# Layer 1 of a four-layer image network on Trainium2: norm sums from 32-column tiles, roots through DRAM rows, and one fold moved from VectorE to GpSimd

## The chip, the cores and the metric

The kernel runs as one program on 1 core of one Trainium2 chip. The metric is device time in microseconds (us) of that core; the number that counts is the median of the runs. Engines are named as in the profile: PE (TensorE matmuls), PEld (its weight loads), DVE (VectorE), ACT (ScalarE), POOL (GpSimd) and SP (SyncE, which issues nearly all DMAs here).

## The reference, cut to what matters

Sixteen images of 96 channels and 56 x 56 pixels pass four layers. Only layer 1 is touched. B = 16, C = 96, Din = 192, L = 3136 pixels.

```
z  = transpose(x)                              # pixels x channels
u  = LN(z) * g + b;  u = u @ in_proj_w.T       # norm 1, 96 -> 192 channels
uc = silu(depthwise_conv3x3(u))
# four directions k: rows, columns, and both reversed
dt = softplus(dts @ dt_w + dt_b);  a = exp(dt * A)
h  = scan(a, dt * B * x)                       # h[t] = a[t] h[t-1] + ...
y  = h * C + D * x
ym = y0 + reverse(y2) + turn(y1 + reverse(y3)) # "turn" swaps rows and columns
z  = z + LN(ym) @ out_proj_w.T                 # out norm, 192 -> 96
m  = LN(z);  z = z + gelu(m @ fc1 + b1) @ fc2 + b2
out = x + z
```

Each of the three norms subtracts a mean over the channels and divides by a root of a variance over the channels.

## The kernel before, in words

Layer 1 is written as small generator tasks. Each step yields an `Op` with an engine, an estimated cost, and the buffers it takes and gives; `in_order` then places the steps one by one, always the one that could start first by these estimates, ties by a rank. The result is a fixed order of instructions on every engine; on the chip each engine works through its own order and waits on semaphores where its operands aren't ready. SP's and POOL's queues are such orders too.

Five task families run beside each other over the 16 images. `front` (rank 3b - 9) makes the first norm, the projection, the convolution (L1107) and the step projections (`p_x`, L1144, whose copy to `proj` at L1146 marks the end of a front). `made_of` (rank -100) makes the step sizes: `p_d` (L1174) on PE, then three ACT passes (L1181, L1183, L1190), and loads the rows `bc` (L1203). `scanned` (rank 99) is DVE's backbone: for 24 pieces of 784 columns a product (L1262), a product into PSUM (L1265), a scan (L1271 or L1273) and a product with C (L1226), and for a third of them L1229. `additions` (rank -1) adds the pieces on POOL (L1295). `back` (rank 3b) makes the out norm, the output projection, the second norm and the MLP in 7 groups of 448 pixels.

The steps that the change touches:

- Norm 1 (`sums` in `front`): per 448 pixels the pixels are the *weights* and a 96-column block of ones is streamed, so that a pixel's sum lies on its own partition (L1035 for x, L1036 for its square from L1029; DVE picks one column, L1038). After L1044 and L1045 POOL takes the power -1/2 (L1047, 112x28). The root is turned back to rows by 28 transposes with a broadcast root as weights (L1057), and DVE multiplies x by it (L1062).
- Channels 128 to 191 of two directions share one tile: partitions 0 to 63 hold rows, 64 to 127 the turned direction. At the end of `sums` of `scanned`, four DVE additions fold the turned half in (L1300, 64x784 each).
- Out norm (`group` in `back`): squares on ACT (L1317, L1319), then per 112 pixels `p_o` from the image as weights: the projection (L1324, L1325, whose 97th column is the mean) and the sum of squares against 96 columns of ones (L1327). ACT copies `p_o` (L1332), DVE makes the variance (L1340, L1341), POOL the root (L1343, 112x4), DVE multiplies (L1350) and adds `p_y` = x + bias (L1347, L1352).
- Second norm: ACT squares (L1357), DVE sums z (L1359) and the squares (L1361), POOL takes the root (L1366). After the MLP, `p_g` (L1392, L1393) is added (L1395) and SP writes 112 x 4 rows of 384 bytes (L1397).

An fp32 matmul appears as two records in the profile, each with a weight load of its own; a transpose as one.

Of the kernel before, what the change touches and what calls it, by code (L numbers as in the profile page):

```python
# [163 lines left out]

class Phase:
# [60 lines left out]
def in_order(buffers, tasks, load=None):  # L226
# [8 lines left out]
    def advance(ready, task, parent, root):  # L235
        nonlocal count
        while True:
# [9 lines left out]
            elif isinstance(got, list):  # L247
                up = [task, len(got), parent, ready]
                for child in got:
                    advance(ready, child, up, root)  # L250
                return
            elif isinstance(got, int):
                ranks[root] = got
            else:
                waiting.append((ready, ("ps" not in got.give, ranks[root], count), task, parent, got, root))
                count += 1
                return
# [3 lines left out]
    while waiting:  # L261
        best = None
        for i, (ready, rank, _, _, op, _) in enumerate(waiting):
            start = max(ready, engines.get(op.engine, 0.0))
            if op.engine == "ACT" and op.table and op.table != tables.get("ACT"):
                start = max(ready, engines.get("ACT", 0.0) + change["ACT"])
# [5 lines left out]
            if best is None or (start, rank) < best[:2]:  # L272
                best = (start, rank, i)
        start, _, i = best
        assert start < np.inf, "the tasks hold all buffers"
        _, _, task, parent, op, root = waiting.pop(i)
# [560 lines left out]
def layer1(ctx, tc, src, given, dst, flags=None, soft=False):  # L837
# [6 lines left out]
    buffers = {  # L844
        "ps": 3, "x": 1, "half": 1, "xc": 2, "big": 7, "proj": 2, "dt": 3, "a": 2, "bc": 3, "hc": 1, "xn": 1,
        "ysq": 1, "o": 2, "z": 2, "zn": 2, "zt": 1, "hid": 1, "xr": 3,
    }
# [28 lines left out]
    ones = ph.c([P, 3, C], "ones")  # L876
# [57 lines left out]
    for i in range(2):  # L934
# [11 lines left out]
        rows.append(ph.c([C1, C], f"rows{i}"))  # L946
        nc.vector.tensor_copy(rows[i], p[:C1, 0, :C])
# [4 lines left out]
    nc.vector.memset(w_out[:, 0, C:], 1.0 / DIN)  # L952
    nc.vector.memset(w_out[:64, 1, C:], 1.0 / DIN)
    for j, n in enumerate((P, 64)):
# [5 lines left out]
        nc.vector.tensor_copy(w_out[:n, j, :C], p[:n, 0, :C])  # L960
    b_fc1 = ph.c([P, 3], "b_fc1")
# [28 lines left out]
    def pe(n, each, take=("ps",), give=(), **k):  # L990
        return Op("PE", n * each, 0.25, take, give, **k)

    def dve(n, each=1.04e-3, over=0.15, **k):
        return Op("DVE", over + n * each, **{"lag": 0.06, **k})

    def act(n, each=0.83e-3, over=0.22, **k):
        return Op("ACT", over + n * each, **k)

    def front(b, it):

        def loaded(g):
            n = min(896, L - 896 * g)
            x = buf([C, 896], "xc")[:, :n]
            nc.sync.dma_start(x, given[b][:, 896 * g : 896 * g + n])
            return x
# [15 lines left out]
        me = work.tile([Q, 8, NT], F32, tag="me", name="me")  # L1021

        def sums(g):
            yield Op("SP", 0.3, 4.0, take=("xc",))
            x = loaded(g)
            for i in range(x.shape[1] // T):
                yield act(T, take=("xn",))
                sq = buf([C, 2, T], "xn")[:, 0]
                nc.scalar.activation(sq, x[:, T * i : T * i + T], AF.Square)  # L1029
                last = i == x.shape[1] // T - 1  # L1030
                yield pe(8, 0.2, give=("xn", "xc") if last else ("xn",))
                p = pair("p_s", P)
                for q in range(4):
                    at = T * i + Q * q
                    nc.tensor.matmul(p[:Q, q, :C], x[:, at : at + Q], ones[:C, 0], start=True, stop=True)  # L1035
                    nc.tensor.matmul(p[:Q, 4 + q, :C], sq[:, Q * q : Q * q + Q], ones[:C, 0], start=True, stop=True)  # L1036
                yield dve(8, give=("ps",))
                nc.vector.tensor_copy(me[:, :, 2 * g + i : 2 * g + i + 1], p[:Q, :, 0:1])  # L1038

        yield [sums(g) for g in range(4)]  # L1040
        v, r = (work.tile([Q, 28], F32, tag=n, name=n) for n in ("v", "r"))
        yield dve(0, over=0.6)
        own = lambda a: a.rearrange("p (g q) -> p q g", q=4)
        nc.vector.scalar_tensor_tensor(own(v), me[:, :4], -1.0, me[:, :4], ALU.mult, ALU.mult)  # L1044
        nc.vector.scalar_tensor_tensor(own(v), own(v), EPS, me[:, 4:], ALU.add, ALU.add)  # L1045
        yield Op("POOL", 6.2)
        nc.gpsimd.tensor_tensor(r, v, nhalf, ALU.pow)  # L1047

        def projected(g):
            banks = 2 if g < 3 else 1  # L1050
            yield Op("SP", 0.3, 4.0, take=("xc",))
            x = loaded(g)
            yield pe(4 * banks, 0.1, ("ps", "xn"))
            p = pair("p_r")
            for q in range(4 * banks):
                at = 8 * g + q
                nc.tensor.transpose(  # L1057
                    p[:C, q // 4, Q * (q % 4) : Q * (q % 4) + Q], r[:, at : at + 1].to_broadcast([Q, C]), ident[:Q, :Q]
                )
            yield dve(448 * banks, give=("ps", "xc"))  # L1060
            xn = buf([C, 2, T], "xn")[:, :banks]
            nc.vector.tensor_tensor(xn, x.rearrange("c (b n) -> c b n", n=T), p[:C, :banks, :T], ALU.mult)  # L1062
# [148 lines left out]
    def scanned(it):  # L1211
# [66 lines left out]
        def sums():  # L1278
            for unit in units:
# [4 lines left out]
                for s in ((1, 0) if back else (0, 1)):  # L1284
# [9 lines left out]
                    yield Op("POOL", 1.9, give=("hc",))  # L1294
                    nc.gpsimd.tensor_tensor(out, out, hc, ALU.add)  # L1295
            ym = it["y"][1]
            for g in range(4):
                yield dve(L / 4, 1.85e-3)
                own = image(ym[:64])[:, 14 * g : 14 * g + 14]
                nc.vector.tensor_tensor(own, own, turned(ym[64:])[:, 14 * g : 14 * g + 14], ALU.add)  # L1300

        it["sums"] = sums()
        yield from scan()

    def back(b, it):

        y0, ym = it["y"]

        def group(g):
# [5 lines left out]
            yield act(T, take=("ysq",))  # L1315
            sq = buf([P, 2, T], "ysq")
            nc.scalar.activation(sq[:, 0], y0[:, cols], AF.Square)  # L1317
            yield act(T)
            nc.scalar.activation(sq[:, 1], ym[:, cols], AF.Square)  # L1319
            yield pe(16, 0.2, ("ps", "o"), ("ysq",))  # L1320
            p = pair("p_o", P)
            for q in range(4):
                own = slice(T * g + Q * q, T * g + Q * q + Q)
                nc.tensor.matmul(p[:Q, q, :C1], y0[:, own], w_out[:, 0], start=True, stop=False)  # L1324
                nc.tensor.matmul(p[:Q, q, :C1], ym[:, own], w_out[:, 1], start=False, stop=True)  # L1325
                for j in range(2):
                    nc.tensor.matmul(  # L1327
                        p[:Q, 4 + q, :C], sq[:, j, Q * q : Q * q + Q], ones[:, 1 + j], start=j == 0, stop=j == 1
                    )
            yield act(4 * C)  # L1330
            o = buf([Q, 4, C1], "o")
            nc.scalar.copy(o, p[:Q, :4, :C1])  # L1332
# [4 lines left out]
            small = lambda n: work.tile([Q, 4], F32, tag=n, name=n, bufs=3)  # L1337
            v, r = small("v4"), small("r4")
            yield dve(0, over=0.4, give=("ps",))
# [538 lines left out]
```

## Time and profile before

| what | value |
|---|---|
| runs (us) | 7140.94, 7140.69, 7134.35; median 7140.69 |
| profiled execution | 7114.45 us, its span 7112.6 us |
| layer 1 in the trace | first sums at 1164.0 us, last output DMA issued at 4417.1 us |
| ends of the fronts (L1146), first and last of 16 | 1281.6 us and 4085.3 us |
| the same in the settled part: six ends, five distances | 2958.9 us to 3897.6 us, so 187.7 us an image |
| granted PE clock over the span | 0.92 |

A busy share is that of the whole span, over four layers. For this change only layer 1 counts, about 3250 us of the span, and in it the settled part from 2200 us to 3950 us, where every image repeats the same order. [...]how fast PE gets on is read from the distance between the starts of neighbouring records.

### The profile page before, as it was taken

To read this page: it belongs to the slowest core of one execution; us is meant where nothing else is said; L and a number is where in the kernel's file an instruction comes from. 1 tells how busy PE (TensorE), PEld (TensorE's weight loads), DVE (VectorE), ACT (ScalarE), POOL (GpSimd) and SP (SyncE) were. 2 spreads that over 40 slices of the span, in tenths; PEclk is the share of its full clock that TensorE was granted. 3 is DMA by queue.
4 is the path that set the end of the run, shared out by engine and by line. 5 is a ranking of instruction groups with operands and counts; after the bars stand their busy time and mean duration, and the time that the engine had idled before them with its cause. 6 is when DMAs were issued, how large, how long until landed. Compare 5 with 4: busy or idle time off the path is not lost. (4 is left out here: it accounts for less than half of the span.)

```text
span 7112.6 us, 114994 instructions
## 1 busy us (share of the span) xinstructions
PE 6280.9 (88%) x46587; PEld 4500.6 (63%) x46587; DVE 5446.3 (77%) x7392; ACT 4546.6 (64%) x6035; POOL 1446.6 (20%) x994
## 2 busy tenths in 40 slices
PE   7999998888889999999999987788999999999986
PEld 3444444445655655556555555687888888888875
DVE  6786884677888888888888885667777777777775
ACT  4454542676777777777777763455666666666664
POOL 0000000132323333333333332111111111111110
PEclk9999998788899999999999988899999999999997
DMA  1111111343444444444444442445555455555542
GB/s 38 31 38 32 40 33 38 110 123 117 124 127 124 127 127 130 127 137 127 128 131 130 126 122 76 96 107 125 130 115 126 112 128 118 121 135 118 119 105 61
DMA packets 495422, 743.56 MB, mean 105 GB/s; under 512 B 199969, under 2 KB 330785, under 8 KB 491570
## 3 DMA queue, kind: packets, MB, share of 16 engines
q1 hardware_dynamic: 493858, 733.25, 39.9%
q8 instruction: 370, 6.06, 0.4%
q0 software_dynamic: 1024, 2.85, 0.1%
q14 instruction: 170, 1.39, 0.1%
HBM read 543.98 MB, written 191.99 MB: 103 GB/s over the span
## 5 line engine op out<-in xcount | busy, mean ns | idle before, releaser
L1578 POOL TENSOR_TENSOR r<-v,nhalf 112x16 f32<-112x16 f32 (+1 forms) x128 | 397.0, 3108 | 2241.5 <-DVE v L1576 1680.7
L1295 POOL TENSOR_TENSOR big<-big,hc 128x784 f32<-128x784 f32 x256 | 537.2, 2099 | 901.9 <-DVE hc L1226 815.2
L1262 DVE TENSOR_TENSOR dt<-dt,big 128x784 f32<-128x784 f32 x384 | 505.5, 1317 | 176.9 <-ACT a L1190 176.7
L777 DVE SCALAR_TENSOR_TENSOR h<-pad,rows,h 128x1568 f32<-128x1568 f32 x288 | 525.9, 1844 | 3.9
L1174 PE MATMUL p_d<-proj,l_dt 32*128 32x392 f32 x1536 | 388.3, 590 | 96.6 <-ACT hid L1384 69.1
L1181 ACT ACTIVATE dt<-p_d,l_dtb 128x784 f32<-128x784 f32 x384 | 350.0, 912 | 128.2 <-PE p_d L1174 110.6
L1636 PE MATMUL p<-k_f,z 112*128 112x112 f32 x3072 | 373.9, 282 | 63.9 <-DMA z<-d 57.5
L1636 PEld LDWEIGHTS p<-k_f,z 112*128 112x128 f32 x3072 | 369.2, 198 | 72.4 <-issue 59.1
L1684 PE MATMUL p_v<-w,gg 128*112 128x97 f32 x2048 | 377.3, 267 | 38.3 <-DVE gg L1670 12.3
L1107 PE MATMUL p_c<-x,taps 64*64 64x392 f32 x4608 | 400.7, 498 | 3.7 <-ACT big L1128 2.7
L1265 DVE TENSOR_TENSOR drive<-dt,bc 128x784 f32<-128x784 f32 x384 | 395.0, 1029 | 11.1 <-DMA bc<-bc 1.0
L1392 PE MATMUL p_g<-l_fc,hid 128*112 128x96 f32 x2688 | 386.1, 285 | 11.8 <-ACT hid L1384 9.4
L1128 ACT COPY big<-p_c 64x392 f32<-64x392 f32 (+1 forms) x448 | 267.3, 599 | 189.7 <-PE p_c L1107 184.1
L1392 PEld LDWEIGHTS p_g<-l_fc,hid 128*112 128x112 f32 x2688 | 347.2, 200 | 51.0 <-ACT hid L1384 24.6
L1685 PE MATMUL p_v<-w2both,gg 128*112 128x97 f32 x2048 | 375.5, 266 | 0.0
L1226 DVE TENSOR_TENSOR hc<-a,bc 128x784 f32<-128x784 f32 x384 | 371.3, 967 | 0.3 <-POOL big L1295 0.2
L1183 ACT ACTIVATE dt<-dt,one 128x784 f32<-128x784 f32 x384 | 363.6, 947 | 7.2
L1382 PE MATMUL p_f<-zt,w_fc 96*128 96x448 f32 x672 | 320.1, 594 | 47.6 <-ACT dt L1181 18.8
L1190 ACT ACTIVATE a<-dt,aneg 128x784 f32<-128x784 f32 x384 | 352.1, 939 | 4.5 <-DVE a L1273 3.1
L750 PE MATMUL p_c<-pad,taps 64*64 64x392 f32 x4032 | 348.8, 495 | 1.8 <-DVE y L816 1.4
L1273 DVE TENSOR_TENSOR_SCAN a<-a,drive 128x784 f32<-128x784 f32 x192 | 350.3, 1824 | 0.1
L1271 DVE TENSOR_TENSOR_SCAN a<-a,drive 128x784 f32<-128x784 f32 x192 | 350.0, 1823 | 0.0
(339 smaller groups left out, 16005.2 us busy)
## 6 DMA issues: line engine op xcount, KB each, us to landing
bc<-bc SPq DMA_DIRECT2D x256, 784.0 KB
bc<-bc SPq DMA_DIRECT2D x256, 392.0 KB
d<-y SPq DMA_DIRECT2D x448, 192.0 KB
z<-d SPq DMA_DIRECT2D x128, 672.0 KB
d<-uu SPq DMA_DIRECT2D x256, 169.8 KB
z<-d SPq DMA_DIRECT2D x192, 194.0 KB
xc<-x SPq DMA_DIRECT2D x96, 336.0 KB
x<-in_x SPq DMA_DIRECT2D x16, 1176.0 KB
```

The source lines that it names most:

```text
L777: nc.vector.scalar_tensor_tensor(out, view, taps9[:, i : i + 1], out, ALU.mult, ALU.add)
L1107: nc.tensor.matmul(p[to : to + 64, b, :TC], taps[64 * s : 64 * s + 64, j, k], pad[64 * s : 64 * s + 64, r0 : r0 + 7, k % 3 : k % 3 + S], s ...
L1174: nc.tensor.matmul(p[:, b, :TC], wdt[on, i], proj[on, h], start=True, stop=True)
L1226: nc.vector.tensor_tensor(hc, a, t[:, 1], ALU.mult)
L1262: nc.vector.tensor_tensor(as_own(dt), as_own(dt), own(u), ALU.mult)
L1265: nc.vector.tensor_tensor(b, dt, t[:, 0], ALU.mult)
L1295: nc.gpsimd.tensor_tensor(out, out, hc, ALU.add)
L1392: nc.tensor.matmul(p[:Q, q, :C], hid[:, j, own], fc2[:, j], start=j == 0, stop=False)
L1578: nc.gpsimd.tensor_tensor(r, v, nhalf[:, :n], ALU.pow)
L1636: nc.tensor.matmul(p[:, q, :Q], flat[:, P * (3 * q + k) : P * (3 * q + k) + P], f2, start=True, stop=True)
L1684: nc.tensor.matmul(out, gs[2 * h][:, at + k], w["w2"][:, 2 * h], start=True, stop=False)
L1685: nc.tensor.matmul(out, gs[1][:, at + k], w["w2both"][:, h], start=False, stop=True)
```

## The change

What it does:

- Norm 1 becomes a task family of its own (`normed`). The ones are now the *weights*, 32 columns wide, and the pixels are streamed: four matmuls, each into another 32 partitions of PSUM, take four quarters of 896 pixels. ACT squares the mean, DVE subtracts it from the mean square (`spread`), a DMA writes one partition of each quarter to a row in DRAM. When a whole image's row is there, it is loaded as 112 x 28, POOL takes the power, and it is written back as a row. In `front` a DMA broadcasts 896 roots to 96 partitions, and the 28 transposes are gone.
- The out norm's sums are made the same way for a whole image (`spreads`, four pieces of 784 pixels, from 128 and then 64 partitions), with one load, one POOL power of 112 x 28 for an image, instead of 7 of 112 x 4. `p_o` holds the projection alone; its pixels are taken four apart (`each`), so that a partition holds four neighbouring pixels and the roots come in pieces of 16 bytes. The image's pixels `x` are taken in the same way for `p_y` and `p_g`. The output is written in pieces of 1536 bytes.
- The 97th column of the weights now holds their row sums, so that the sum of z comes with the products and DVE's sum (L1359) is gone, as is ACT's copy (L1332).
- The fold of the turned half is made by POOL, piece by piece, as soon as a piece is complete; a DMA first moves 64 x 784 values from partitions 64 to 127 to partitions 0 to 63.
- The planner gets leads for some pairs of engine and task (subtracted from or added to a step's start when the next one is chosen), other ranks, slightly changed estimates and other numbers of buffers.

The diff, cut to its core:

```diff
+TUNED = {'layer1': {'buffers': {... 'xn': 1, 'ysq': 1, 'vr': 1, 'fold': 1, 'xr1': 1, 'z': 2, 'zn': 1, 'xr': 2},
+            'leads': {('PE', 'spreads'): -1.4, ('PE', 'steps'): -3.4, ('SP', 'sums'): -0.4, ('ACT', 'hidden'): -0.7,
+                      ('SP', 'norms'): 2.5, ('POOL', 'fronts'): -0.9, ('POOL', 'backs'): -0.6, ('SP', 'projected'): -2.9,
...
+            'hold': 0.3, 'norm': -6, 'front': -6, 'back': -3, 'make': -100, 'scan': -50, 'chains': 3}}
...
-            if best is None or (start, rank) < best[:2]:
-                best = (start, rank, i)
+            if best is None or (start + key, rank) < best[:2]:
+                best = (start + key, rank, i, start)
...
-    ones = ph.c([P, 3, C], "ones")
+    ones = ph.c([P, 3, 32], "ones")
...
     def pe(n, each, take=("ps",), give=(), **k):
-        return Op("PE", n * each, 0.25, take, give, **k)
+        return Op("PE", 1.05 * n * each, 0.25, take, give, **k)
...
+    def spread(mean, square, out, n):
+        yield act(n, take=("vr",))
+        t = buf([P, 224], "vr")[:, :n]
+        nc.scalar.activation(t, mean, AF.Square)
+        yield dve(n, give=("ps",))
+        nc.vector.scalar_tensor_tensor(t, t, -1.0, square, ALU.mult, ALU.add)
+        yield Op("SP", 0.3, 3.0)
+        nc.sync.dma_start(out.rearrange("o (q n) -> (o q) n", q=4), t[::32])
...
+        def sums(g):          # in normed
...
+            for k, a in enumerate((x, sq)):
+                for q in range(4):
+                    nc.tensor.matmul(p[32 * q : 32 * q + 32, k, :n], ones[:C, 0], a[:, n * q : n * q + n], start=True, stop=True)
+            yield from spread(p[:, 0, :n], p[:, 1, :n], var[:, 896 * g : 896 * g + 4 * n], n)
+        yield [sums(g) for g in range(4)]
...
+        nc.sync.dma_start(v, whole_of(var))
+        nc.vector.tensor_scalar(v, v, EPS, None, ALU.add)
+        nc.gpsimd.tensor_tensor(r, v, nhalf, ALU.pow)
+        nc.sync.dma_start(whole_of(it["root"]), r)
...
         def projected(g):
-            for q in range(4 * banks):
-                nc.tensor.transpose(p[:C, q // 4, Q * (q % 4) : Q * (q % 4) + Q], r[:, at : at + 1].to_broadcast([Q, C]), ident[:Q, :Q])
+            nc.sync.dma_start(rb, it["root"][:, 896 * g : 896 * g + n].to_broadcast([C, n]))
+            nc.vector.tensor_tensor(xn.rearrange("c b n -> c (b n)"), x, rb, ALU.mult)
...
-            for g in range(4):
-                yield dve(L / 4, 1.85e-3)
-                nc.vector.tensor_tensor(own, own, turned(ym[64:])[:, 14 * g : 14 * g + 14], ALU.add)
+        def folded():
+            for k in (3, 2, 1, 0):
+                yield Op("none", 0.0, 0.0, wait=folds[k])
+                yield Op("SP", 0.3, 3.0, take=("fold",))
+                nc.sync.dma_start(t, ym[64:, SUB * k : SUB * k + SUB])
+                yield Op("POOL", 1.9, give=("fold",))
+                nc.gpsimd.tensor_tensor(own, own, t.rearrange("p (w h) -> p w h", h=S), ALU.add)
...
+        def spreads(g):       # in back
+            nc.scalar.activation(sq, y0[:, cols], AF.Square)
+            nc.scalar.activation(ym[64:, cols], ym[:64, cols], AF.Square)
+            yield pe(4, n * 1.7e-3, give=("ysq",))
+            for k, (full, part, on) in enumerate(((y0[:, cols], ym[:64, cols], slice(0, 64)), (sq, ym[64:, cols], slice(64, P)))):
+                for i in range(2):
+                    for q in range(4):
+                        nc.tensor.matmul(p[32 * q : 32 * q + 32, k, :n], (ones[:, 1], ones[on, 1])[i], (full, part)[i][:, own], start=i == 0, stop=i == 1)
+            yield from spread(p[:, 0, :n], p[:, 1, :n], var[:, cols], n)
...
+        nc.gpsimd.tensor_tensor(r2, v2, nhalf, ALU.pow)
+        each = lambda t, q: t.rearrange("c (p q) -> c q p", q=4)[:, q]
...
-                nc.tensor.matmul(p[:Q, q, :C1], y0[:, own], w_out[:, 0], start=True, stop=False)
-                nc.tensor.matmul(p[:Q, q, :C1], ym[:, own], w_out[:, 1], start=False, stop=True)
-                for j in range(2):
-                    nc.tensor.matmul(p[:Q, 4 + q, :C], sq[:, j, Q * q : Q * q + Q], ones[:, 1 + j], start=j == 0, stop=j == 1)
-            nc.scalar.copy(o, p[:Q, :4, :C1])
+                nc.tensor.matmul(p[:Q, q, :C1], each(y0[:, cols], q), w_out[:, 0], start=True, stop=False)
+                nc.tensor.matmul(p[:Q, q, :C1], each(ym[:64, cols], q), w_out[:64, 1], start=False, stop=True)
...
-                nc.tensor.matmul(p[:Q, q, :C], x[:, Q * q : Q * q + Q], rows[0], start=True, stop=True)
+                nc.tensor.matmul(p[:Q, 4 + q, :C1], each(x, q), rows[0], start=True, stop=True)
...
-            nc.vector.tensor_reduce(s1, z, AX.X, ALU.add)
...
-                nc.tensor.matmul(p[:Q, q, :C], x[:, own], rows[1], start=False, stop=True)
+                nc.tensor.matmul(p[:Q, q, :C], each(x, q), rows[1][:, :C], start=False, stop=True)
...
-        in_order(buffers, [fronts(), makes(), scans(), additions(), backs()], None if soft else one_set)
+        in_order(buffers, [norms(), fronts(), makes(), scans(), additions(), backs()], None if soft else one_set, tuned["hold"], tuned["leads"])
```

## The prediction

> **What bounds the kernel now.** I read four views in this order. First the slices of the page. Each slice is 178 us; layer 1 fills slices 7 to 25.
>
> ```profile
> PE   7999998888889999999999987788999999999986
> DVE  6786884677888888888888885667777777777775
> PEclk9999998788899999999999988899999999999997
> ```
>
> PE stands at nine tenths, DVE at eight: PE is nearest to full, DVE next. Then the windows of the settled part (us, then busy us with instructions for PE, PEld, DVE, ACT, POOL, then PE clock, DMA share, GB/s).
>
> ```profile
> 2800.00:2990.00 190.00, 175.44 (x1338) 114.21 (x1338) 165.14 (x203) 148.46 (x195) 65.50 (x48) 0.93 0.45 128
> 2990.00:3180.00 190.00, 174.84 (x1334) 113.76 (x1335) 165.31 (x200) 148.57 (x197) 64.78 (x47) 0.93 0.46 131
> ```
>
> Over six periods of 187.7 us (2818 to 3944 us) an image costs PE 173.1 us, DVE 163.1, ACT 146.2, POOL 63.2. PE idles 14.6 us of each 187.7. What DVE waits for in those six periods:
>
> ```profile
> DVE z L1395 <- PE p_g L1393: 56.8, 36, 4.1
> DVE dt L1262 <- ACT a L1190: 41.1, 18, 3.6
> ```
>
> Both lead back to PE: `p_g` is PE's own, and L1190 stands behind `p_d`. So the period is PE's work plus a remainder that waits leave. Third, the groups of instructions, shapes apart, which I price from.
>
> ```profile
> L1327 PE MATMUL p_o<-ones,ysq 128*112 128x96 f32 x1792 | 286.9, 287 | 19.8 <-ACT ysq L1319 15.5 <-ACT ysq L1317 4.2
> L1035 PE MATMUL p_s<-ones,xc 96*112 96x96 f32 x896 | 193.6, 304 | 30.8 <-DMA xc<-x 17.1 <-ACT zt L1375 7.0 <-ACT hid L1384 4.3
> L1324 PE MATMUL p_o<-w_out,big 128*112 128x97 f32 x896 | 185.7, 293 | 6.5 <-ACT hid L1384 3.8 <-DVE z L1352 1.6 <-ACT dt L1181 1.1
> L1343 POOL TENSOR_TENSOR r<-v,nhalf 112x4 f32<-112x4 f32 x112 | 156.1, 1394 | 361.6 <-DVE v L1341 361.6
> L1300 DVE TENSOR_TENSOR big<-big 64x784 f32<-64x784 f32 x64 | 102.8, 1606 | 4.8 <-POOL big L1295 2.9
> L1359 DVE TENSOR_REDUCE s<-z 112x4 f32<-112x384 f32 x112 | 60.8, 544 | 0.3
> L1332 ACT COPY o<-p_o 112x388 f32<-112x388 f32 x112 | 53.1, 474 | 152.6 <-PE p_o L1327 152.6
> ```
>
> Last the timeline of the weight loads of `p_x`, because one of its three sets of matmuls streams turned pixels, 224 bytes from each to the next.
>
> ```profile
> 2956.22 0.13 PEld L1144 LDWEIGHTS p_x<-big,l_xw 128*32 128x32 f32 x4 [0.20 <-issue]
> 2956.55 0.13 PEld L1144 LDWEIGHTS p_x<-big,l_xw 128*32 128x32 f32 x4 [0.20 <-issue]
> 2957.26 0.15 PEld L1144 LDWEIGHTS p_x<-big,l_xw 128*32 128x32 f32 x4 [0.58 <-issue]
> 2957.98 0.16 PEld L1144 LDWEIGHTS p_x<-big,l_xw 128*32 128x32 f32 x4 [0.56 <-issue]
> ```
>
> Four records run side by side, one per 32 columns. A set of 392 contiguous columns takes 0.33 us (0.84 ns a column), a turned one 0.71 us (1.82 ns).
>
> **What the Trainium skill says.** "TensorE: Matmul & The Clock Gate", LDWEIGHTS: P / 1.2 ns for P columns, so 93 ns for 112. The starts of L1324 to L1327 lie 0.098 us apart at full clock: it agrees, and these records are bound by the weight load. "TensorEngine Tiling (Array Packing)", Key Properties: a change of tiling drains the array. The setup agrees: at half clock a pair of L957 from 64 rows amid pairs from 128 takes 0.67 us against about 0.43. "SBUF — State Buffer", Door 1: a new 16-byte line costs, and one can stride for free up to "4 fp32"; its Specifications ask for two hits a line. The first reading makes the change's stride of four free, the second doesn't; the trace has 224 bytes only. Same page, Who interferes with whom: DVE with two SBUF inputs and POOL exclude each other. The 1317 ns mean of L1262 over its median of 975 is partly that, partly the turned pieces.
>
> **Part by part, per image.**
>
> *PE, removed.* L1327 has 1792/16 = 112 records, L1035 and L1036 112 more. A record costs 0.098 us at full clock and 0.187 at half; a mean clock of 0.93 is 14% of the time at half, so 0.110. 224 x 0.110 = 24.7 us. The 28 transposes L1057 at 0.11: 3.1. Together 27.8 us.
>
> *PE, added.* Norm 1: three pieces of 224 columns and one of 112, two tensors, two passes each: 784 x 4 x 0.84 ns = 2.6 us. Out norm: four pieces of 196, two tensors, two row parts, two passes: 4 x 8 x 196 x 0.84 ns = 5.3. At that clock, 8.6. Changes of tiling (64 against 128 rows: 28 pairs of L1325, 16 in the new sums): between 0 and 0.24 us each, so 0 to 10.6; I take 5.6, about half. Net without the stride: -27.8 + 8.6 + 5.6 = -13.6.
>
> *PE, the stride.* 224 records (L1324, L1325, L1347, L1393) load 112 weights 16 bytes apart. Lower bound 0. Upper bound the turned rate: 112 x 1.82 = 204 ns a record for 110, +21 us. Nothing excludes either; a gain is excluded, as a contiguous load is the fastest shown. I take 0, leaning on the page's "4 fp32", and keep 21 for the first rival.
>
> *DVE.* Removed: L1300 4 x 1.61 = 6.4, L1359 3.8, L1038 7 x 0.164 = 1.1, L1340 and L1341 7 x 0.36 = 2.5, L1044 and L1045 0.3: 14.1. Added: eight `spread` steps; from L1038 (8 elements, 164 ns) and L1359 (384, 544 ns) about 0.37 us for 196 to 224, so 2.9, and two small adds, 0.3. L1062 and L1350 keep their sizes. Net -10.9: 152 us.
>
> *ACT.* L1332 goes (3.3). Squares of 896 or 784 columns instead of 448 save about 1; eight squares of the mean cost about 0.33 each, 2.6. Net about -2.
>
> *POOL.* Seven L1343 go (9.8), one power of 112x28 comes (4.8, as L1047 there), four folds at 2.1 (as L1295): +3.4, a third busy. POOL's order is fixed: behind a fold or power that waits for its DMA stands L1295, and with one buffer `hc` L1226 and DVE wait for that. A piece lasts DVE some 7 us and L1295 2.1, so 4.8 us is hidden once; two such in one piece would not be.
>
> *SP.* Some 58 DMAs an image (8 xc, 36 bc and proj, 14 xr and out) become 77: variance rows 4 + 4, loads 2, root 1, broadcasts 4, folds 4. At about 0.4 us of issue each, 8 us on a queue with room. But each waits for its producer, and behind it stand `bc` loads, for which L1265 waits. Three `bc` buffers are two pieces, 15 us, ahead. I cost it at nothing; if the cover is gone, 1 to 4 us a stall. DMA share rises from 0.45 to about 0.5: root broadcasts move 1.2 MB and folds 0.8 against some 24.
>
> *Latency.* The out norm waits for row, load, power: some 20 us, while `y` holds two of seven large buffers. Now the last L1324 ends some 39 us ahead of the convolution that wants them: covered. At the two ends of the layer it is bare: +16 us in all, an estimate from DMA steps of 2.7 us and the power.
>
> *The order.* The lead of 3.4 us for `p_d` may spare part of DVE's 41.1/6 = 6.9 us a period. I count 0; it is the low end.
>
> **Sum.** PE 173.1 - 13.6 = 159.5, plus the same idle 14.6: 174.1 us, DVE 87% busy as before, so it need not bind. 15 periods x 13.6 = 204, less 16: -188 us. Against the profiled execution, 7114.45 (span 7112.6 and 1.9 around it): 6926. Its time lies 26 below the median shown; I carry the difference, not the level: 7140.7 - 188 = 6953.
>
> **Rivals.**
>
> *Strided weights load at half rate* (ends slower). Place: L1324, L1325, L1347, L1393. Price 21 us an image against 13.6 gained; it decides from 13.6 x 1000/224 = 61 ns a record, two thirds of the bound. Full: +7.4 x 15 + 16 = +127: 7268. For it: the turned set doubles, and the specification's two hits. Against: that stride is fourteen lines and on the streaming side.
>
> *In-order waits eat the gain.* SP or POOL waits stall DVE or PE some four times an image for 3 us: 12 x 15 = 180 back, 7133. For it: 19 more DMAs, two of them chained through DRAM. Against: `bc` waits cost DVE nothing now (1.0 us in 384 at L1265).
>
> *The better order also pays.* PE idles 8 instead of 14.6 us, DVE at 90%: another 6 x 15 = 90, 6863. It would need DVE's waits at L1262 and L1395 to halve.
>
> **Chances.** Forecast 0.47 (its own range 6900 to 7010, tiling and idle a few us an image either way), better order 0.15, strided weights 0.27, waits 0.11 (half of it within the bound, a quarter on each side). A measurement here can tell 0.2%, 14 us, from no change. Faster 0.47 + 0.15 + 0.03 = 0.65, the same 0.05, slower 0.30. The 80% range runs from 6860 to 7265.
>
> **What would show it.** Right: settled period 172 to 176 us; neighbouring starts of the new L1324 still 0.10 us apart; no records like L1327; DVE busy about 152 an image. Strided: those starts 0.2 us apart at full clock and PE busy above 175 an image. Waits: idle time before L1265 or L1226, released by DMA or POOL. I am wrong in kind if the period falls below 165 (PE wasn't the bound) or layers 0, 2 and 3 move.

## The result and the profile after

The changed kernel takes 7834.8 us (median of 4 runs, 7829.5 to 7856.6) against 7138.9 us before: a ratio of 1.098, 95% interval 1.096 to 1.100. I had forecast 6953, and the range ended at 7265. The difference arises in layer 1: from the first weights loaded for the next layer to the end, the traces have 2682 us before and 2679 after.

The slices of the page of after, in tenths; a slice is now 196 us, and layer 1 fills slices 7 to 27:

```profile
PE   7999987599899999999899998868899998999986
DVE  6787783856666766666666668437777877777765
PEclk9999997577777777777777776679999999999997
```

PE is as full as before. DVE went from eight tenths to six, and the clock granted to PE from nine tenths to seven. So PE got slower, not busier. The windows of five images of the settled part, before and then after (us, then busy us with instructions for PE, PEld, DVE, ACT and POOL, then PE clock, DMA share, GB/s):

```profile
2451.00:3394.00 943.00, 867.83 (x6592) 562.05 (x6591) 817.15 (x992) 732.08 (x960) 316.73 (x230) 0.93 0.45 129
2673.00:3868.00 1195.00, 1098.49 (x6295) 635.21 (x6294) 802.13 (x872) 725.11 (x916) 339.28 (x221) 0.75 0.39 111
```

A period (the time from one image to the next) is 1195/5 = 239 us, where it was 943/5 = 188.6. DVE works 160 us of it, nearly what it worked before (163), and waits the rest. What it waits for there (us in total, times, longest):

```profile
DVE z L1478 <- PE p_g L1476: 118.9, 25, 9.3
DVE z L1432 <- PE p_o L1429: 100.1, 35, 6.4
DVE dt L1322 <- ACT a L1250: 81.5, 25, 5.1
```

The first and the last are the two long waits of before (9.5 and 6.9 us an image there), now at 24 and 16 us, and `p_o` is new among the long ones. The groups of instructions of the new output matmuls (L1421, L1422 and L1429 were L1324, L1325 and L1347):

```profile
L1422 PE MATMUL p_o<-w_out,big 64*112 64x97 f32 x896 | 311.3, 440 | 0.0
L1421 PE MATMUL p_o<-w_out,big 128*112 128x97 f32 x896 | 304.8, 433 | 4.9 <-ACT dt L1241 4.7 <-ACT hid L1467 0.2
L1429 PE MATMUL p_o<-rows,xr 97*112 97x97 f32 x896 | 210.9, 410 | 2.7 <-POOL xr L1416 2.7
```

L1324 had 185.7 us for the same 896 records; L1421 has 304.8. How that comes about is seen in PE's timeline at full clock. A row holds records of one line that follow each other, and its first number is the start of the first. Before, then after:

```profile
2750.20 0.36 PE L1325 MATMUL p_o<-w_out,big 128*112 128x97 f32 x2
2750.39 0.56 PE L1327 MATMUL p_o<-ones,ysq 128*112 128x96 f32 x4
2750.78 0.36 PE L1324 MATMUL p_o<-w_out,big 128*112 128x97 f32 x2
```

```profile
2856.68 0.65 PE L1421 MATMUL p_o<-w_out,big 128*112 128x97 f32 x2
2857.26 0.65 PE L1422 MATMUL p_o<-w_out,big 64*112 64x97 f32 x2
2857.83 0.65 PE L1421 MATMUL p_o<-w_out,big 128*112 128x97 f32 x2
```

Two records took 0.19 us before; now pairs start 0.57 to 0.58 us apart. So a record costs 0.28 to 0.29 us where it cost 0.098.

**How the table further down is made.** From the trace of five settled images of each kernel I take, line by line, the number of PE records times the mean distance from one start to the next at full clock. The sum is PE's *work*. PE's busy time minus the work is what the half clock adds (*clock*); the rest of the period is *idle*. (L1393 of after and e3 never ran at full clock; half of its 0.101 us stands for it.) Before: 188.6 = 159.2 + 14.4 + 15.0. After: 238.9 = 176.5 + 43.1 + 19.3. Of the 50 us more, 17 are work, 29 clock and 4 idle.

### The profile page after: what moved, and what is told of

It is laid out like the page before. It is cut to its first block, busy times and chain, and to the rows that moved or that the text cites. A ratio compares the mean times of both kernels' runs of the same rounds, so it can differ in the third digit from the quotient of the medians.

```text
span 7833.6 us, 113202 instructions
## 1 busy us (share of the span) xinstructions
PE 6924.9 (88%) x45627; PEld 4674.4 (60%) x45627; DVE 5388.2 (69%) x7010; ACT 4508.8 (58%) x5881; POOL 1523.8 (19%) x962
## 5 line engine op out<-in xcount | busy, mean ns | idle before, releaser
L1322 DVE TENSOR_TENSOR dt<-dt,big 128x784 f32<-128x784 f32 x384 | 484.0, 1260 | 258.2 <-ACT a L1250 258.2
L1234 PE MATMUL p_d<-proj,l_dt 32*128 32x392 f32 x1536 | 454.5, 681 | 167.5 <-ACT hid L1467 106.2
L1475 PE MATMUL p_g<-l_fc,hid 128*112 128x96 f32 x2688 | 501.0, 344 | 2.4 <-ACT hid L1467 2.0
L1475 PEld LDWEIGHTS p_g<-l_fc,hid 128*112 128x112 f32 x2688 | 450.9, 254 | 51.3 <-ACT hid L1467 33.2
L1465 PE MATMUL p_f<-zt,w_fc 96*128 96x448 f32 x672 | 389.3, 716 | 78.6 <-ACT zt L1458 61.2
L1167 PE MATMUL p_c<-x,taps 64*64 64x392 f32 x4608 | 441.1, 537 | 0.2
L1325 DVE TENSOR_TENSOR drive<-dt,bc 128x784 f32<-128x784 f32 x384 | 425.3, 1107 | 8.8 <-issue 0.3
L1234 PEld LDWEIGHTS p_d<-proj,l_dt 32*128 32x128 f32 x1536 | 141.7, 226 | 397.4 <-ACT hid L1467 159.3
L1695 PE MATMUL p_a<-first,xt 97*112 97x192 f32 x1792 | 337.4, 336 | 17.3 <-ACT xt L1689 6.8
L1333 DVE TENSOR_TENSOR_SCAN a<-a,drive 128x784 f32<-128x784 f32 x192 | 350.5, 1825 | 0.5
```

The costliest lines, as they stand in the source:

```text
L1167: nc.tensor.matmul(p[to : to + 64, b, :TC], taps[64 * s : 64 * s + 64, j, k], pad[64 * s : 64 * s + 64, r0 : r0 + 7, k % 3 : k % 3 + S], s ...
L1234: nc.tensor.matmul(p[:, b, :TC], wdt[on, i], proj[on, h], start=True, stop=True)
L1322: nc.vector.tensor_tensor(as_own(dt), as_own(dt), own(u), ALU.mult)
L1325: nc.vector.tensor_tensor(b, dt, t[:, 0], ALU.mult)
L1465: nc.tensor.matmul(p[:, 0, :T], w_fc1[:, P * j : P * j + P], zt, start=True, stop=True)
L1475: nc.tensor.matmul(p[:Q, q, :C], hid[:, j, own], fc2[:, j], start=j == 0, stop=False)
```

## The experiments

### The stride and the rows: e1 to e4, e8

The first theories: S, the weights that lie 16 bytes apart; T, tiles that change between 64 and 128 rows; P, the new order.

```diff
# e1 (and e4): neighbouring pixels as weights
-        each = lambda t, q: t.rearrange("c (p q) -> c q p", q=4)[:, q]
+        each = lambda t, q: t[:, Q * q : Q * q + Q]
# e3 (and e4): 128 rows in the second matmul
-                nc.tensor.matmul(p[:Q, q, :C1], each(ym[:64, cols], q), w_out[:64, 1], start=False, stop=True)
+                nc.tensor.matmul(p[:Q, q, :C1], each(ym[:, cols], q), w_out[:, 1], start=False, stop=True)
# e2: the kernel before, so too at L1325, L1347 and L1393
+        each = lambda t, q: t.rearrange("c (p q) -> c q p", q=4)[:, q]
-                nc.tensor.matmul(p[:Q, q, :C1], y0[:, own], w_out[:, 0], start=True, stop=False)
+                nc.tensor.matmul(p[:Q, q, :C1], each(y0[:, cols], q), w_out[:, 0], start=True, stop=False)
```

> The changed kernel with one edit: the 112 pixels of p_o, p_y and of the last matmul of p_g are neighbours again instead of four apart. The pixels then meet the roots of other pixels, so this part of the computation is changed; instructions, order and DMAs are the same. Theory S (strided weight loads, by their own time and by leaving PE so little work per time that its clock is granted at half): starts of L1421, L1422, L1429 and L1476 at full clock 0.10 us apart, PE clock in the settled part back from 0.76 to above 0.88, period from 237 us to 180 to 195, total 7000 to 7250 us. Theory T (the small tiles, 32 columns wide and 64 rows high, drain the array and lower the clock): direct time falls by some 20 us an image, the clock stays below 0.82, total 7450 to 7600. Theory P (the new order with its leads is worse): total above 7450, and the clock back.

> The kernel before with one edit: the weights of L1324, L1325, L1347 and of the last matmul of p_g are taken four pixels apart, 224 records an image; L1327 keeps its neighbours, so that its sums belong to other pixels and the order of the output pixels is changed. Theory S: these records 0.2 us apart at full clock, PE clock in the settled part from 0.93 to below 0.85, period from 188 us to 215 to 240, total 7550 to 7950 us. Theories T and P: only the loads' own time, 224 x 0.1 = 22 us an image at most, clock 0.90 or more, total 7140 to 7500.

> The changed kernel with one edit: the second matmul of p_o takes all 128 partitions again (rows 64 to 127 of its other operand are zeros), so that p_o no longer alternates between 128 and 64 rows. Theory T: starts of L1421 and L1422 from about 0.28 to 0.205 us apart, 112 x 0.075 = 8 us an image and some of the clock, total 7450 to 7700. Theory S: the same 8 us at most, clock still below 0.80, total 7680 to 7830. Theory P: 7800 or more.

> Both edits on the changed kernel: neighbouring pixels as weights (roots of other pixels, as in the first run) and 128 rows for the second matmul of p_o. Theory S with my prediction's sum: period 170 to 180 us, total 6900 to 7050 us, clock 0.90 or more. Theory T: much below the first run, by 300 us or more. Theory P: above the kernel before although PE has less to do.

Measured: e1 7560.9, e2 7352.8, e3 7632.0, e4 7323.9, beside 7147.1 for before on that chip. PE's timelines at full clock, of e1, e3 and e4:

```profile
2755.01 0.44 PE L1421 MATMUL p_o<-w_out,big 128*112 128x97 f32 x2
2755.38 0.43 PE L1422 MATMUL p_o<-w_out,big 64*112 64x97 f32 x2
2755.74 0.44 PE L1421 MATMUL p_o<-w_out,big 128*112 128x97 f32 x2
```

```profile
2776.40 0.58 PE L1422 MATMUL p_o<-w_out,big 128*112 128x97 f32 x2
2776.82 0.58 PE L1421 MATMUL p_o<-w_out,big 128*112 128x97 f32 x2
2777.23 0.58 PE L1422 MATMUL p_o<-w_out,big 128*112 128x97 f32 x2
```

```profile
2830.28 0.36 PE L1422 MATMUL p_o<-w_out,big 128*112 128x97 f32 x2
2830.48 0.36 PE L1421 MATMUL p_o<-w_out,big 128*112 128x97 f32 x2
2830.67 0.36 PE L1422 MATMUL p_o<-w_out,big 128*112 128x97 f32 x2
```

Halved, the distances are 0.18 us with rows that alternate, 0.21 with the stride alone, 0.098 with neither, 0.28 with both. So the stride adds 0.107 us to a record and the alternation some 0.08, and they add up. The alternation's price isn't one of the change alone: in e1 the two records of one matmul, between which the rows stay the same, start 0.174 us apart, and 0.19 where the rows change. In e2, where nothing else changes, 224 such records add 183.0 - 159.2 = 23.8 us of work, the period grows by 16, and the run is slower by 206 us. So both the stride and the alternation cost PE time, and they aren't enough: e4 has neither and is still 177 above before, as P had put it. S had also expected the stride to pull the clock down by itself; e2's stayed at 0.92, so that part fell, and with it S's totals for e1, e2 and e3. T's ranges held for these three, but e4 came out 237 below e1, where T had asked for 300.

e8 takes the 64 rows out of the out norm's sums as well.

```diff
# e8: e4 with all 128 rows in L1393; zeros in the weights mask the rows that don't belong
-            for k, (full, part, on) in enumerate(((y0[:, cols], ym[:64, cols], slice(0, 64)), (sq, ym[64:, cols], slice(64, P)))):
+            for k, (full, part, on) in enumerate(((y0[:, cols], ym[:, cols], 2), (sq, ym[:, cols], 3))):
```

> The kernel of e4 (roots of other pixels) with 128 rows in all of the out norm's sums: zeros in the weights mask the rows that do not belong, so that no 64-row matmul is left in the settled part. Theory U: 7050 to 7200, clock 0.89 or more. Theory P: within 60 of e4 (7265 to 7385). Theory C: as P or a little less.

It gave 7248.0, 76 less than e4, between the two theories. The lines of L1393 in one image of after and of e4, then of the same records (L1394) in one image of e8 (records, ns least/median/most):

```profile
L1393 PE MATMUL p_v<-big,ones x96: 531/532/536, 2921.6 to 2940.8; 64*32 64x196 f32 x64, 128*32 128x196 f32 x32
L1393 PE MATMUL p_v<-big,ones x96: 531/532/536, 2938.6 to 2957.8; 64*32 64x196 f32 x64, 128*32 128x196 f32 x32
```

```profile
L1394 PE MATMUL p_v<-big,ones x96: 328/329/536, 2888.7 to 2902.6; 128*32 128x196 f32 x96
```

In after every record of this line ran at half clock, in all five images. In e4, which differs from e8 in these rows alone, about a quarter of the records of five images ran at full clock, and in e8 three quarters.

### The order: e5, e6, e7, e9, e11

```diff
# e5: e4 without leads and hold; e6: also the old ranks and estimates
-        in_order(buffers, [norms(), fronts(), makes(), scans(), additions(), backs()], None if soft else one_set, tuned["hold"], tuned["leads"])
+        in_order(buffers, [norms(), fronts(), makes(), scans(), additions(), backs()], None if soft else one_set)
# e7: the kernel before with the diff's in_order, leads, hold, ranks and estimates
# e9: e8 with these buffers; to make room, the folded rows lie in the squares' buffer
-                        'zn': 1,
+                        'zn': 2,
-                        'xr': 2},
+                        'xr': 3},
-                t = buf([64, SUB], "fold")
+                t = buf([P, SUB], "ysq")[:64]
# e11: e8, and eight such lines more
-                    yield pe(1, 0.75)
+                    yield pe(1, 0.95)
```

> The kernel of e4 (neighbouring pixels as weights, so the roots belong to other pixels, which changes that part of the computation; 128 rows in the second p_o matmul) with the leads and the hold taken out of the rule that orders the work; ranks and cost estimates as after. Left to explain: e4 takes 7324, 371 more than my forecast and 177 more than the kernel before. Theory P (the order): the leads put PE's work where it waits; without them 7150 to 7200 or less. Theory U (small sums): the sums with 32 columns and 64 rows let the granted clock fall, whatever the order; then 7300 to 7350 here. Theory C (PE with less work per time lowers its own clock): 7300 to 7400, as nothing fills PE here.

> e5 with the ranks (norms and fronts 3b - 9, backs 3b, scans 99) and the estimates of durations of the kernel before as well; so all of the change's work without its stride and its 64-row p_o matmul, in the old order (roots belong to other pixels, as in e4). Theory P: 6950 to 7100, clock 0.90 or more, DVE idle below 28 us an image. Theory U: 7280 to 7350, clock 0.87. Theory C: the same as U.

> The kernel before with nothing changed but the order: ranks, leads, hold and duration estimates of the kernel after. Theory P: slower than before by 150 to 400 (7300 to 7550), with a granted clock near 0.87. Theories U and C: within 60 of before (7090 to 7200), clock 0.92, as PE has the old work.

> e8 (roots of other pixels) with the buffers of the kernel before for the three output chains: zn two, xr three (after: one and two); the folded rows share the space of the squares to make room, and the planner orders anew. In e8 PE waits 11.7 us an image for the transposes of zn. Theory B (the chains hold each other up by one zn): that wait falls below 5 us, PE idles under 20 us an image, 7050 to 7150. Theory I (idle time comes from the order as a whole, and half clock from idle time): 7150 to 7350, either sign.

> e8 (roots of other pixels) ordered with durations as e8's trace shows them (nine estimates changed: dt times B 1.2 ns a column, x times root 2.1, additions 2.15 us, folds 2.7, p_f 1.1, p_d 0.95, the small matmuls 0.245 us), leads kept. Theory O (the plan's wrong durations cause the idle time): 7050 to 7170. Theory I (the plan's fit is fragile but not a matter of these estimates): 7180 to 7400.

Measured: e5 7552.1, e6 7658.3, e7 7483.7 (before there 7137.7); e9 7574.4, e11 7233.7 (before there 7135.8). P fell as I had put it: the new order is not worse, it is worth 334 us to the new work (e6 against e4). On the old work it costs 346, as P expected there. Each order fits the work that it comes with. For e5, e6 and e9 every range that I had put down was too low. In e7 PE's work hardly changes (155.7 us), but idle time doubles to 33 us and the half clock adds 34 where it added 14. In e9 the wait that was to go did go, and others came; the shared buffer of the folded rows and the squares is a part of that edit, and wasn't tried apart. Waits of PE over five images, in e8 and then in e9:

```profile
PE p_d L1235 <- ACT hid L1468: 42.1, 15, 4.0
PE p_t L1456 <- DVE zn L1452: 38.5, 11, 4.6
```

```profile
PE p_d L1235 <- ACT hid L1468: 34.2, 17, 4.4
PE p_d L1235 <- DVE vr L1052: 22.2, 10, 6.1
PE p_f L1466 <- DVE z L1437: 17.1, 9, 3.3
```

PE's idle time ahead of the transposes fell from 11.5 to 2.3 us an image, its idle time in all rose from 28.8 to about 40. Better estimates (e11) moved the time by 14 us, where theory O had asked for at least 78: it fell.

### The clock and the work: e10, e12

```diff
# e10: e8, ahead of each group's transposes of zn
+            for _ in range(2):
+                nc.tensor.matmul(p[:C1, 1, :T], w_out[:, 0], filling, start=True, stop=True)
# e12: the kernel before; sums for the first of four sets of pixels only, shared by the other three
-                for j in range(2):
+                for j in range(2 if q == 0 else 0):
```

> e8 (roots of other pixels) with two matmuls of 448 columns that nobody reads ahead of each group's transposes of zn, where PE waits most: 14 a image, 1.5 us a group, 10.5 us of added PE work an image at full clock, order of the rest unchanged. Theory H (a window in which PE idles lowers the clock, and the lowered clock costs e8 some 27 us an image): clock from 0.85 to 0.90 or more in the settled part, time 7050 to 7250, no slower than e8 in spite of the added work. If the clock does not follow PE's idle time: the added work shows, 7300 to 7400.

> The kernel before with three quarters of its sums on PE left out (each four pixels' columns share the first one's mean of squares, so the roots are wrong): 84 of 112 records of L1327 and 84 of 112 of L1035 and L1036 an image; same planned order, nothing else changed. By my prediction's step (PE's work at 0.110 us a record comes off the period): 168 x 0.110 = 18.5 us an image, 6860. Theory I (DVE's 163 us and the waits between the engines hold the period; the freed time turns to idle time and half clock): 6990 to 7140.

e10: 7262.7. The windows of five images of e8, of e10 and of e12:

```profile
2473.00:3476.00 1003.00, 858.69 (x6295) 493.18 (x6293) 805.75 (x871) 724.29 (x916) 348.47 (x221) 0.84 0.47 132
```

```profile
2475.00:3482.00 1007.00, 877.47 (x6434) 493.83 (x6430) 799.44 (x871) 724.48 (x916) 331.63 (x221) 0.89 0.46 131
```

```profile
2392.00:3318.00 926.00, 816.48 (x5744) 487.19 (x5743) 814.67 (x991) 732.84 (x960) 317.34 (x230) 0.89 0.46 132
```

11.3 us of added work an image raised PE's busy time by 3.8 us and the period by 0.8. The half clock's share fell from 29.5 to 22.0 us: the clock does follow PE's idle time, and the higher clock paid for the added work. It bought no time, though; PE's idle time fell by 3 us only.

e12: 7024.5, 1.5% below before (ratio 0.985, 0.983 to 0.986). The order is untouched and 15.9 us of work an image are gone, yet the period fell by 3.4 us only; idle time took 6.9 and the clock 5.6. The whole run gained 111 us, a part of it at the ends of the layer, of the 277 that my way of counting promised.

### One wait at a time: e13 to e18

```diff
# e13: no folds
-                nc.sync.dma_start(t, ym[64:, SUB * k : SUB * k + SUB])
-                nc.gpsimd.tensor_tensor(own, own, t.rearrange("p (w h) -> p w h", h=S), ALU.add)
# e14: nhalf in place of r2 as factor of z    e15: z[:, q] in place of zn[:, q] in the transposes
# e16: a constant tile in place of rb    e18: e13 to e16 together
# e17: e8 with the folds on DVE, the four steps of the kernel before
```

> e8 (roots of other pixels) with the folds left out: neither their four DMAs nor their four additions on GpSimd, so the turned half is missing in the output; planned order unchanged. Theory W1 (the folds hold GpSimd's fixed order and the out norm back): 7100 to 7170. Theory I (no single one of the new waits; the order as a whole): 7200 to 7250.

> e8 with z multiplied by a constant in place of the out norm's root (the root is still computed, by nobody read), so that no output group waits for the sums, their rows in DRAM and the power; order unchanged. Theory W2 (the groups used to start one by one and now wait for the whole image's root): 7080 to 7170. Theory I: 7200 to 7255.

> e8 (roots of other pixels) with the transposes reading z in place of zn, so that the second norm is left out of the output and PE doesn't wait for its sums, its power and its product (11.5 us an image stand ahead of these transposes); order unchanged. Theory W3 (this wait is what keeps PE idle and cold): PE idle 18 us, 7020 to 7120. Theory I (another wait comes next): 7150 to 7240.

> e8 (roots of other pixels) with the first norm's product taken with a constant tile in place of the root's row from DRAM: four broadcasts an image fewer and no wait for them (roots are still computed and stored); order unchanged. Theory W4 (rows through DRAM stall the fronts and SP's queue): 7100 to 7170. Theory I: 7200 to 7255.

> e8 (roots of other pixels) with the turned half folded in by DVE as in the kernel before (four steps at 1.6 us, after all of GpSimd's additions), so that part of the change is undone; the planner orders anew. The folds cost e8 some 82 us as e13 shows. If what they cost is GpSimd's fixed order, this gets most of it back: 7170 to 7220, DVE 6 us an image busier. If DVE's time holds the period as much as GpSimd's, 7230 to 7350.

> e13 (no folds) with the three other waits gone as well: constant in place of the out norm's root, transposes from z, constant in place of the first norm's row (so the output lacks the folds, both norms' roots and the second norm); order unchanged. Theory I (the order as a whole holds the rest): 7080 to 7160, PE idle above 22 us an image, clock below 0.90. If the waits cover each other, so that only all four together count: below 7000, PE idle under 16 us.

Measured: e13 7165.6, e14 7254.8, e15 7234.7, e16 7246.6 (before there 7142.5); e17 7399.8, e18 7096.0 (before there 7137.2). Only the folds gave anything alone, 82 us. Putting them on DVE, in a new order, lost 152; after e9 I can't say how much of that is the fold and how much the new order. That is above both ranges that I had put down for e17. In e15 PE still idled 28.5 us an image, though its wait ahead of the transposes had fallen from 11.5 to 3.0. The three others together gave 70 more on top of e13 where alone they gave -7, 13 and 1, so they do cover each other. All four gave 152 us, where the second theory wanted 250. What PE waits for in e18:

```profile
PE p_d L1237 <- ACT hid L1467: 35.0, 12, 4.0
PE p_f L1465 <- ACT zt L1458: 22.5, 10, 2.6
PE p_f L1465 <- DVE vr L1052: 17.0, 5, 3.6
```

The long wait ahead of `p_d` stays whatever is taken away: e8, e13 to e16 and e18, all in one order, have 34 to 42 us of it in five images. As I read the kernel, PE's next matmul needs a PSUM pair, and ACT has yet to read `p_f` out of it; no run gave PE another pair.

### The main runs in one table

Us; the four right columns are of one settled image, from the traces. Ratios are to before on the same chip.

| kernel | median | ratio (95%) | period | work | clock | idle |
|---|---|---|---|---|---|---|
| before | 7138.9 | | 188.6 | 159.2 | 14.4 | 15.0 |
| e2 before, stride | 7352.8 | 1.029 (1.027 to 1.030) | 204.8 | 183.0 | 10.1 | 11.7 |
| e7 before, new order | 7483.7 | 1.048 (1.047 to 1.050) | 222.3 | 155.7 | 34.0 | 32.6 |
| e12 before, fewer sums | 7024.5 | 0.985 (0.983 to 0.986) | 185.2 | 143.3 | 20.0 | 21.9 |
| after | 7834.8 | 1.098 (1.096 to 1.100) | 238.9 | 176.5 | 43.1 | 19.3 |
| e1 no stride | 7560.9 | 1.058 (1.056 to 1.061) | 222.7 | 152.6 | 47.9 | 22.2 |
| e3 128 rows in `p_o` | 7632.0 | 1.068 (1.066 to 1.070) | 227.9 | 165.2 | 41.9 | 20.8 |
| e4 both | 7323.9 | 1.024 (1.022 to 1.026) | 204.7 | 143.3 | 35.1 | 26.3 |
| e8 e4, 128 rows in the sums | 7248.0 | 1.016 (1.015 to 1.018) | 200.6 | 142.3 | 29.5 | 28.8 |
| e10 e8, filled waits | 7262.7 | 1.018 (1.016 to 1.020) | 201.4 | 153.6 | 22.0 | 25.9 |
| e13 e8 and no folds | 7165.6 | 1.003 (1.002 to 1.004) | 194.6 | 142.0 | 27.3 | 25.3 |
| e18 e13 and three waits gone | 7096.0 | 0.995 (0.993 to 0.997) | 191.5 | 143.6 | 22.5 | 25.3 |

## Why the prediction was wrong

The step that failed first is the stride, put at 0; after it come the alternating rows, and PE's half clock and idle time, carried over as constants. None of them alone turned the direction: without the stride the kernel is still 5.8% slower than before (e1), without stride and alternation 2.4% (e4). In medians, down the table, the 882 us between forecast and result are: stride 274 (after to e1), alternating rows 237 (e1 to e4), 64 rows in the sums 76 (e4 to e8), folds 82 (e8 to e13), the three waits together 70 (e13 to e18), and 143 that are left between e18 and 6953. Taken in another order the terms shift (rows first: 203, then the stride 308), and the chips differ by up to 11 us.

- **"I take 0, leaning on the page's '4 fp32'"** failed. The trace of before had nothing of this stride, so I chose between two readings of the Trainium skill. "SBUF — State Buffer", Door 1, calls a stride of four fp32 free; its Specifications ask for two hits on a 16-byte line for full bandwidth. The second is right here: 0.205 us for 112 weights with one hit a line, 0.098 with four. The bound of +21 us an image was the value to take: e2 adds 23.8 us of work.
- **"Changes of tiling": 5.6, bound 10.6.** The place was right, and the total was at the bound: 9.3 us of work for `p_o` (e1 less e4) and 1.0 for the sums. That the bound held is luck: its 0.24 a pair allows `p_o` 6.7 and the sums 3.8. The cost goes with each record while the rows alternate, not with a change alone, as the 0.174 us above show.
- **"Plus the same idle 14.6" at "a mean clock of 0.93"** is the miss in kind. I carried both over as constants and priced every PE record with them. The clock is a result: after runs at 0.75, and that alone adds 29 us a period, more than the added work. "TensorE: Matmul & The Clock Gate", in "What's actually happening", says that the clock is halved by default and that windows of about 3.4 us of activity release it; the half-clock stretches in the traces last 3.41 us and multiples. In before (2200 to 3950 us) the clock fell after 46 windows, each with PE busy under 75%, and never after the 375 windows with more. In after it fell 72 times, 30 of them after a window with PE busy over 95%, and three quarters of those windows' time is L1421 and L1422. With alternation alone it is 13 of 69 (e1), with the stride alone 26 of 74 (e3); in e4, with neither, no such fall is left (63 of 63 came under 75%), nor in e2, where the strided records stand between others. The same from the other side: of the full-clock windows that L1421, L1422 and L1429 fill to more than 70%, with PE busy over 75%, all 26 are followed by half clock in after, 13 of 27 in e1, 19 of 40 in e3, and none of 25 in e4. So stretches whose records start late don't hold the clock, though the profile shows PE busy. That PE counts as idle while it waits for its weights is my reading; what the clock goes by wasn't measured itself. And this is the smaller part of the 29 us: without stride and alternation e4 still has 35.1 us of half clock, to 43.1 in after and 14.4 in before, and each of its 63 falls came after a window with PE busy under 65%.
- **"PE stands at nine tenths ... so the period is PE's work plus a remainder".** Without stride and alternation, PE's work fell as the sum says: from 159.2 to 142.3 us in e8, and the sum without tiling changes (-19.2 at 0.110 us a record) is some -17 at full clock. But e12 shows what such a fall is worth in the old kernel itself, with nothing else touched: 15.9 us of work gave 3.4 us of period. The freed time went to PE's idle time and half clock. That DVE, at 163 of 188.6 us, and the fixed orders that tie it to PE through ACT hold the period is the likely reason, which would make my "need not bind" wrong; no run took work off DVE in an unchanged order, so it is not shown.
- **DVE -10.9** came out at -3.0 (163.4 to 160.4). Three lines grew by some 7.7 us an image in the two windows of five images, nearly all of the missing 7.9: L1445, which took L1362's place, L1122 (before: L1062) and L1325 (before: L1265). In each, most instances run as before and a few take far longer:

```profile
L1362 DVE SCALAR_TENSOR_TENSOR v<-s 112x4 f32<-112x4 f32 x112 | 19.8, 177 | 0.0
L1445 DVE SCALAR_TENSOR_TENSOR v<-z 112x4 f32<-112x4 f32 x112 | 56.5, 505 | 0.0
```

Of L1445, 30 of 112 take 1.5 us on average and the rest 0.16 (L1362: 2 such in 112); of L1122's large ones 12 of 48 take 2.9 us where all of L1062 took 1.08; of L1325 28 of 384 take 2.7 us (L1265: 12). POOL was at work in every one of these 70, and in 86 of the other 474. The prediction names this collision of DVE and POOL for L1262 and prices it for no other line. It is read from that coincidence; no run took POOL away from these lines.
- **Folds behind L1295 "hidden once".** They cost 5 to 6 us an image in e8. A fold takes 2467 ns, not 2.1 us.
- **"Latency +16", "SP: nothing"** were not contradicted one by one: e14 and e16 gave -7 and 1 us, within what a run tells. Together with the transposes' wait, and without folds, these waits were worth 70 us (e13 to e18).
- **"The order: I count 0; it is the low end".** It was bounded on the good side only. e7 shows what a reordering can cost.

Among the rivals, "Strided weights load at half rate" had the place and the price right (+21 us) but not its consequences; 7268 was the case nearest to the result. "In-order waits eat the gain" is the kind of thing that is left at the end, 143 us; e12 shows the same in the old kernel, where 166 of 277 us were eaten. What holds these 143 us was not found; it isn't the four waits that were tried alone and together. No version here was run that beats the kernel before with its whole computation.

## What to carry to other kernels

Before weights are re-laid, look for one row with that stride in the trace; without one, take the bad end, since a stride of 16 bytes doubled what these small matmuls cost. Don't carry the clock over as a constant: price PE at full clock, and ask which windows of 3.4 us will fall under three quarters of real work once records are gone or start late. And where two engines stand within a tenth of each other in fixed orders, don't book work taken off one as time gained: here (e12) most of it turned into idle time and half clock.

## What the runs showed of the hardware

- Records with 112 fp32 weights 16 bytes apart start 0.205 to 0.207 us apart at full clock and 0.20 to 0.207 at half clock (medians of `p_o` in e2 and e3): they don't follow PE's clock. Without a stride it is 0.098 and 0.187.
- While 64 and 128 rows alternate from matmul to matmul, records start 0.18 us apart at full clock, against 0.098 for 128 rows throughout, with and without a change between the two. With the stride as well it is 0.28 to 0.30.
- PE busy over 95% in the records can still lose the clock, where these records start 0.18 to 0.29 us apart (30 of 72 falls in after).
- 14 unread matmuls an image, placed where PE waits, raised the granted clock from 0.84 to 0.89 and lengthened the period of 200 us by 0.8.
- A DVE instruction of 0.16 us took 1.5 us in 30 of 112 cases, each time with POOL at work (L1445 in after).
